# Layer 1's input loaded one layer earlier, and its queries, keys and norms moved from two-bank to one-bank PSUM tiles, in a four-layer network of four images

## The chip, the core and the metric

The kernel runs on one core of one Trainium2 chip. Five engines work in it, each through its own list of instructions in order: PE (matmuls; PEld is its weight loads), DVE, ACT, POOL, and SP, which here only issues DMAs. ACT and POOL issue DMAs too. The metric is the device time of one execution in microseconds (us), as the median of several.

## The reference, cut to what matters

The input is four images of 32 x 32 pixels with 384 channels, in f32. Four layers follow one another, each of them on the group-normalised input (32 groups of 12 channels) and added to it:

```
x = x + L0(gn(x))   # deformable attention: offsets from a convolution, samples of the
                    # image gathered at the offsets, 6 heads over 1024 x 1024 positions
x = x + L1(gn(x))   # 12 heads of 32 channels:
                    #   q, k, v = x Wqkv;  xg = x Wg;  gc = strided 3x3 convolution of xg
                    #   sim = sigmoid(l2norm(xg) . l2norm(gc)),  w = sim sim^T
                    #   softmax(q k / sqrt(32)) * (gamma w + 1 - gamma), renormalised, times v
x = x + L2(gn(x))   # ratio of windowed sums
x = x + L3(gn(x))   # 3x3 local attention: weights from x Wa, values x Wv, folded back
```

## The kernel before, in words

P is 128 partitions, N the 1024 positions of an image, KC = 3 blocks of 128 channels, NJ = 8 blocks of 128 positions.

**Two streams.** `Front` is layer 0, `Trunk` layers 1 to 3 of an image. Both are Python generators that yield a weight after each piece of work. Layer 0 of image 0 runs alone. Then `Net.layer3` drives `Trunk.image(b)` and, by the weights, lets layer 0 of image b+1 advance beside it (1109 units of trunk against 714 of front, with a lead of 0.1). With image 3 there is no front left. This gives the order in which the instructions are written; a scheduler then orders each engine's list by its own estimate of when operands come, except those pinned with `keep_in_program_order` (the first heads, and in a gather the first multiply and the first transpose).

**PSUM.** `big()` gives tiles of two banks, of which there are two buffers; `bank()` gives tiles of one bank, of which there are four. Front and trunk share both. `weights()` (L237) loads a 128 x 3 x 384 weight into one of three buffers.

**Layer 1's inputs** (`inputs1`, from L1059). x is loaded by three DMAs of SP (L1063). The norm takes statistics on DVE (L306, L307), sums them over groups on PE with one-column matmuls (L330, once for the means `gn_mv`, once for the variances `gn_d`) and writes xh (L357). The product with Wg goes by `dense_t` (L376: six matmuls of 512 columns into a big) to the padded tile xp (L1076), from which DVE makes the strided convolution. `queries_keys(ko)` makes one block of q and one of k by `dense_t`, each in a big, copied out whole (L1101 on ACT, L1103 on DVE) and stored to DRAM (L1104). Squares are summed over heads (L1131) and inverted. `sums_step(i)` (L1246, L1254, L1255) makes the maximum and the sum of exponentials of pair 0's softmax for one block of rows; it uses both bigs: matmuls, reduction on DVE, exponential on ACT. The norms (L1158, L1166, L1172) take a big and a bank for each ko, the values (L390, L1110) a bank. `sums_finish` and `load_lse` bring the sums to DRAM and back.

**Layer 1's pairs** (`pair`, six for an image). `sims` makes sim in its own tile (L1285, L1292); then for each of eight blocks POOL scales a part of it to sg (L1350), PE makes q k into a big (L1365), ACT its exponential (L1373), PE the group weights from sim and sg and the transposes of earlier blocks (L1395, L1390), ACT copies what later blocks need (L1403), DVE multiplies (L1404), PE multiplies with the values (L1339).

**Layers 2 and 3.** `layers23` keeps x in a tile of its own. `out1` loads it on ACT's queue (L1438) and adds the projection (L1450, L1462). Layer 2 keeps three tiles d (L1503). Layer 3 has its own xh; each of eight blocks of weights goes to DRAM (L1660) and back skewed as mt (L1662), even ones on SP and odd ones on ACT. x is transposed by PE (L1671) and copied by ACT into eight tiles y (L1675); then PE multiplies mt with the values (L1683), DVE adds y (L1691) and SP stores (L1692).

**The front's parts that matter here.** sidx (L509) holds the indices of the samples. POOL gathers them with 48 indirect DMAs for an image, in eight groups of six (L667), into three buffers gat; DVE weighs and sums a group (L680, L681, L683, the last reader of gat), PE transposes it (L694). POOL's sg of the trunk stand in the same list as the gathers. The convolution of the offsets is L599, its result copied by L607. The first image's heads (`heads0`, L820 on) are a hand-made software pipeline over 96 blocks, all pinned; AHEAD is how many blocks the scores run ahead of the exponentials, and its tiles win, z and lg have 8, 5 and 23 buffers. In a turn DVE does L885 (z), L890 (lg), L935 (adds the scores), L940 (running maximum) and L954 (subtracts it); PE ends a block with L964.

Of the kernel before, what the change touches and what calls it, by code (L numbers as in the profile page):

```python
# [21 lines left out]
ALU = mybir.AluOpType  # L22
# [4 lines left out]
P = 128  # L27
NB, HW, C = 4, 32, 384
N = HW * HW
# [43 lines left out]
class Net:  # L73


    def __init__(self, ctx, tc, a):
        self.tc, self.nc, self.a = tc, tc.nc, a
        nc = self.nc
        pool = lambda name, bufs, **kw: ctx.enter_context(
            tc.tile_pool(name=name, bufs=bufs, **kw)  # L80
        )
        self.const = pool("const", 1)
        self.wts = pool("wts", 3)
        self.ps2 = pool("ps2", 2, space=PSUM)
        self.ps1 = pool("ps1", 4, space=PSUM)
        self.dram = pool("dram", 1, space=DRAM)
        self.n = 0
        self.consts()
        self.scratch()
        self.front, self.trunk = Front(self, "right"), Trunk(self, "left")  # L90

    def nm(self, base):
# [187 lines left out]
class Lane:  # L280
# [32 lines left out]

    def norm(self, x, out, mv=None):


        nc = self.nc
        if mv is None:
            mv = self.moments()
            for k in range(KC):  # L320
                self.stats(mv, x, k)
        gmat = self.weights("gmat")

# [75 lines left out]
class Front(Lane):  # L399
# [419 lines left out]
    def heads0(self, work):  # L819
# [9 lines left out]

        AHEAD, SUB, OUT = 8, 10, 11  # L830
        win, z, lg, ps, half, dens, inv = {}, {}, {}, {}, {}, {}, {}
# [11 lines left out]
        def divide(step, k):  # L843
# [6 lines left out]
            elif step == 1:  # L850
                pin(v.reciprocal(dens[k], dens[k]))
                for r, h in enumerate(heads):
                    nc.sync.dma_start(by_row(self.rden[h]), dens[k][:, r, :])
                for q in range(2):
                    inv[q] = tile_of([P, HN], "lg", 23)
                    for r, h in enumerate(heads):
                        nc.sync.dma_start(
                            inv[q][r * GC : (r + 1) * GC],
                            self.rden[h][0, q * HN : (q + 1) * HN].partition_broadcast(GC),
                        )  # L860
            else:
                for q in range(2):
                    out = queries(2 * k, q)
                    w = inv[q].rearrange("p (y x) -> p y x", x=HW)
                    pin(v.tensor_tensor(out, out, w, ALU.mult))

        def turn(t):
            i = t + AHEAD

            if i + 5 < n:  # L870
                h, q, j = blocks[i + 5]
                win[i + 5] = tile_of([P, (HH + 1) * WROW], "win", 8)
                nc.gpsimd.indirect_dma_start(
# [19 lines left out]
            if 0 <= i < n:  # L893
                lg[i] = tile_of([P, HN], "lg", 23)
                pin(nc.scalar.activation(
# [5 lines left out]
            if 0 <= i + 1 < n:  # L901
                wv = win[i + 1].rearrange("p (r c) -> p r c", c=WROW)
                z[i + 1] = tile_of([P, HH, HW + 1], "z", 5)
                pin(nc.scalar.activation(
# [87 lines left out]
        for i in range(4):  # L992
            h, q, j = blocks[i]
            win[i] = tile_of([P, (HH + 1) * WROW], "win", 8)
            nc.gpsimd.indirect_dma_start(
# [40 lines left out]
class Trunk(Lane):  # L1036


    def image(self, b, out):
        with self.scope("l1y"):  # L1040

# [17 lines left out]
    def inputs1(self, b):  # L1059
        nc, v = self.nc, self.nc.vector  # L1060
        x = self.wt([P, KC, N], "x")
        for k in range(KC):
            nc.sync.dma_start(x[:, k, :], self.x1[b % 2][k * P : (k + 1) * P, :])  # L1063
        xh = self.wt([P, KC, N], "xh")
        self.norm(x, xh)
        yield 15


# [26 lines left out]

        def queries_keys(ko):
            for w, dst in ((wq, self.qd), (wk, self.kd)):
                ps = self.dense_t(w, xh, ko)
                t = self.wt([P, N], "qk", 2)
                if dst is self.qd:  # L1100
                    nc.scalar.mul(t, ps, HD1**-0.5)  # L1101
                else:
                    v.tensor_copy(t, ps)  # L1103
                nc.sync.dma_start(dst[ko * P : (ko + 1) * P, :], t)  # L1104

# [7 lines left out]

        queries_keys(0)
        self.load_sums(0)
# [23 lines left out]
        nc.scalar.activation(inv[:, N:], psc[0 : KC * 32, 0:M1], AF.Sqrt)  # L1139
        queries_keys(1)  # L1140
        yield 14
        wv = self.weights("Wqkv", 2 * C)
        for part in (inv[:, 0:512], inv[:, 512:]):
            v.tensor_scalar(part, part, 1e-12, None, ALU.max)
            v.reciprocal(part, part)
        self.sums_step(0, st)
        queries_keys(2)
        yield 14
        self.sums_step(1, st)
        yield 10  # L1150
        values(range(NJ // 2))
        self.sums_step(2, st)
        yield 18
        for k in range(KC):
            rows, heads = slice(k * P, (k + 1) * P), slice(32 * k, 32 * k + 32)
            ps, pc = self.big(), self.bank()
            for out, lo in ((ps[:, 0:512], 0), (ps[:, 512:N], 512), (pc[:, 0:M1], N)):
                nc.tensor.matmul(  # L1158
                    out,
                    self.hall[heads, :],  # L1160
                    inv[heads, lo : lo + out.shape[-1]],
                    start=True,
                    stop=True,
                )
            t = self.wt([P, N + M1], "sq", 2)
            v.tensor_tensor(  # L1166
                t[:, 0:N].rearrange("p (y x) -> p y x", y=HW),
                pads[k][:, 1:, 1:],
                ps.rearrange("p (y x) -> p y x", y=HW),
                ALU.mult,  # L1170
            )
            v.tensor_tensor(t[:, N:], raw[:, k, :], pc[:, 0:M1], ALU.mult)  # L1172
            nc.sync.dma_start(self.xgd[rows, :], t[:, 0:N])
            nc.sync.dma_start(self.gcd[rows, :], t[:, N:])
            if k == 0:
                self.load_groups(0)
            self.sums_step(3 + k, st)
            yield 8
        for i in range(2):
            values(range(4 + 2 * i, 6 + 2 * i))  # L1180
            self.sums_step(6 + i, st)
        self.sums_finish(0, st)
        self.load_lse(0)
        yield 28

# [90 lines left out]
    def sims(self, p):  # L1276

        nc = self.nc
        sim = self.wt([P, 2, 2, N], "sim")
        for h in range(2):  # L1280
# [147 lines left out]
    def layers23(self, b, out):  # L1428
        with self.scope("l23"):
            self.x = self.wt([P, KC, N], "x")  # L1430
            yield from self.out1(b)
# [35 lines left out]
    def layer2(self):  # L1467
        nc, v = self.nc, self.nc.vector
        with self.scope("l2"):
# [8 lines left out]
            def squares(k):  # L1478
# [23 lines left out]
                t = self.wt([P, HW, HW + 2], "t", 2)  # L1502
                d = self.wt([P, HW, HW], "d", KC)  # L1503
                v.tensor_tensor(t, sq[:, :, 0 : HW + 2], sq[:, :, 1 : HW + 3], ALU.add)
# [60 lines left out]
    def layer3(self, b, out):  # L1565
        nc, v = self.nc, self.nc.vector
        skew = self.skew[b % 2]
        with self.scope("l3"):
# [209 lines left out]
```

## Time and profile before

| what | us |
|---|---|
| median of three runs | 4804.75 (4781.11 to 4805.06) |
| the profiled execution | 4803.82 |
| its span, from first to last instruction | 4802.0 |
| PE busy, DVE busy, ACT busy, POOL busy | 4201.4, 3136.5, 2411.3, 942.6 |
| mean granted clock of PE | 0.917 of full |

| stretch of the span | what runs |
|---|---|
| 0 to 570 | layer 0 of image 0, alone |
| 570.1 | x of layer 1, image 0, is loaded |
| 1776.2, about 2933, 4030.3 | the same of images 1, 2 and 3 |
| 4030 to 4802 | image 3's layers 1 to 3, without a front |

In the profile's views, "[6.44 <-DMA x<-x]" says that the engine was idle 6.44 us before and that a DMA into x ended it; "x12" is a count of instructions put together in a row. `big<-xh,w` names the tile written and the tiles read. In the table of windows each row is a stretch of time with each engine's busy time in it; PEclk is the clock that was granted to PE, 1.00 being full. A matmul leaves two records, its operands being f32: the counts in the views are of records.

### The profile page before, as it was taken

The page shows a single profiled execution, that of the slowest core. Times are in us where ns is not written, and L with a number is a line of the kernel's source. Part 1 is how long each engine was busy: PE and PEld are TensorE (multiplying, and loading weights), DVE is VectorE, ACT ScalarE, POOL GpSimd, SP SyncE. Part 2 cuts the span into 40 slices and gives each one's busy share as a digit, 9 for nine tenths or more (in the row PEclk, how much of TensorE's full clock was granted, in tenths as well). Part 3 has the DMA queues.
Part 4 walks back from the last instruction along what each step waited for, and adds up shares of the span by engine and source line. Part 5 has one row for each costly group of instructions (what it writes and reads, how often), then busy time and mean ns, then how long its engine had stood idle before and what let it go on. Part 6 is the DMA issues. An engine that isn't in the chain of part 4 may idle for free. (4 is left out here: it accounts for less than half of the span.)

```text
span 4802.0 us, 46610 instructions
## 1 busy us (share of the span) xinstructions
PE 4201.4 (87%) x15704; PEld 1793.1 (37%) x15704; DVE 3136.5 (65%) x5727; ACT 2411.3 (50%) x3693; POOL 942.6 (20%) x946
## 2 busy tenths in 40 slices
PE   5477798999999898899999989799999998999988
PEld 2222243333333353333333444343333334343444
DVE  3599655777877727577778744667686873455544
ACT  2166333666665313566767332456676631466642
POOL 0643104211212102311212110421121210000000
PEclk8689897999999987999999989799999998899998
DMA  6433234222212233321212133431121213201011
GB/s 118 142 102 103 81 101 131 84 60 57 71 40 73 75 116 123 106 57 48 80 50 68 44 100 116 130 98 55 38 77 39 79 47 109 86 25 31 19 39 40
DMA packets 230927, 366.82 MB, mean 76 GB/s; under 512 B 117475, under 2 KB 164672, under 8 KB 230688
## 3 DMA queue, kind: packets, MB, share of 16 engines
q1 hardware_dynamic: 169672, 197.36, 13.9%
q0 software_dynamic: 39936, 145.53, 10.3%
q10 hardware_dynamic: 21080, 20.96, 1.8%
q8 instruction: 124, 2.03, 0.2%
q14 instruction: 115, 0.94, 0.1%
HBM read 285.84 MB, written 78.21 MB: 76 GB/s over the span
## 5 line engine op out<-in xcount | busy, mean ns | idle before, releaser
L1404 DVE SCALAR_TENSOR_TENSOR e<-bank,gam,e 128x512 f32<-128x512 f32 x768 | 558.3, 749 | 571.8 <-ACT gn L1403 276.4
L1395 PE MATMUL bank<-sim,sg 128*128 128x512 f32 (+3 forms) x2304 | 877.4, 515 | 11.6 <-POOL sg L1350 8.9
L1255 ACT ACTIVATE big<-big,nmax 128x1024 f32<-128x1024 f32 x384 | 418.6, 1090 | 395.2 <-DVE nmax L1254 340.2
L1373 ACT ACTIVATE e<-big 128x1024 f32<-128x1024 f32 x384 | 376.9, 1019 | 363.4 <-PE big L1365 358.1
L1395 PEld LDWEIGHTS bank<-sim,sg 128*128 128x128 f32 x2304 | 408.3, 200 | 390.5 <-issue 301.4
L1254 DVE TENSOR_REDUCE nmax<-big 128x1 f32<-128x1024 f32 x384 | 453.5, 1218 | 77.0 <-PE big L1246 34.1
L752 POOL DMA_INDIRECT win<-strips,widx x288 | 308.1, 1070 | 629.2 <-DVE z L765 328.1
L1350 POOL TENSOR_SCALAR sg<-sim,gam 128x512 f32<-128x512 f32 x192 | 148.5, 776 | 1430.8 <-PE bank L1395 1140.7
L1365 PE MATMUL big<-qa,ka 64*128 64x512 f32 x1536 | 414.1, 630 | 14.8 <-ACT big L1255 8.8
L1246 PE MATMUL big<-k,q 32*128 32x512 f32 x1536 | 355.2, 697 | 81.4 <-ACT big L1255 38.2
L667 POOL DMA_INDIRECT gat<-pairs,sidx x192 | 210.1, 1094 | 500.6 <-DVE ix_gt L479 401.7
L773 PE MATMUL bank<-qpad,kz 128*128 128x512 f32 x576 | 283.0, 617 | 15.0 <-DVE e L1404 15.0
L808 PE MATMUL bank<-lg,va 128*64 128x512 f32 x576 | 265.0, 602 | 16.3 <-ACT lg L806 16.2
L808 PE MATMUL bank<-lg,ones 128*64 128x512 f32 x576 | 264.3, 602 | 0.0
L770 DVE SCALAR_TENSOR_TENSOR lg<-z,bias_f,lg 128x512 f32<-128x512 f32 x288 | 227.9, 803 | 40.1 <-ACT lg L769 38.6
L764 ACT ACTIVATE z<-win,bias_f 128x528 f32<-128x528 f32 x288 | 207.1, 739 | 63.3 <-DVE lg L770 39.2
L1365 PEld LDWEIGHTS big<-qa,ka 64*128 64x128 f32 x1536 | 135.5, 189 | 272.4 <-issue 159.3
L765 DVE SCALAR_TENSOR_TENSOR z<-win,bias_f,z 128x528 f32<-128x528 f32 x288 | 216.2, 769 | 27.0 <-DMA win<-strips,widx 16.6
L805 DVE TENSOR_TENSOR lg<-lg,tb 128x512 f32<-128x512 f32 x288 | 187.6, 705 | 51.4 <-ACT tb L798 51.4
L1339 PE MATMUL bank<-e,vs 128*32 128x512 f32 x1536 | 210.9, 605 | 2.1 <-DVE vs L1333 2.1
L769 ACT ACTIVATE lg<-z,bias_f 128x512 f32<-128x512 f32 x288 | 201.4, 720 | 19.1 <-PE bank L808 10.7
L376 PE MATMUL big<-xh,w 128*128 128x512 f32 x432 | 199.3, 619 | 12.2 <-ACT big L1255 10.8
(291 smaller groups left out, 6658.3 us busy)
## 6 DMA issues: line engine op xcount, KB each, us to landing
pairs<-xn SPq DMA_DIRECT2D x64, 192.0 KB
q<-qd SPq DMA_DIRECT2D x48, 256.0 KB
w<-in_gmat SPq DMA_DIRECT2D x16, 576.0 KB
w<-in_w_off SPq DMA_DIRECT2D x12, 576.0 KB
w<-in_Wqkv SPq DMA_DIRECT2D x12, 576.0 KB
a<-in_x SPq DMA_DIRECT2D x16, 384.0 KB
x<-a ACTq DMA_DIRECT2D x4, 1536.0 KB
win<-strips,widx POOLq DMA_INDIRECT x384
```

Of the source, the lines that this page charges most:

```text
L752: nc.gpsimd.indirect_dma_start(out=win, out_offset=None, in_=self.strips[:, :], in_offset=bass.IndirectOffsetOnAxis(ap=self.widx[:, q, c : ...
L765: v.scalar_tensor_tensor(z, wv[:, 1 : HH + 1, 0 : HW + 1], sc(0, 1), z, ALU.mult, ALU.add)
L770: v.scalar_tensor_tensor(lg, z[:, :, 1 : HW + 1], sc(0, 0), lg, ALU.mult, ALU.add)
L773: nc.tensor.matmul(ps, kz[:, j * P : (j + 1) * P], both, start=True, stop=True)
L808: nc.tensor.matmul(po[out, :], w, lf, start=j == 0, stop=j == NJ - 1)
L1246: nc.tensor.matmul(ps[r][:, h * 512 : (h + 1) * 512], self.q4[rows, i * P : (i + 1) * P], self.k4[rows, 0:512], start=True, stop=True,)
L1254: v.tensor_reduce(nmax[:, r, i : i + 1], ps[r], AX.X, ALU.max, negate=True)
L1255: nc.scalar.activation(ps[r], ps[r], AF.Exp, bias=nmax[:, r, i : i + 1], accum_out=den[:, r, i : i + 1],)
L1365: nc.tensor.matmul(ps[:, r, :], ka[rows, j * P : (j + 1) * P], qa[rows, cols], start=True, stop=True,)
L1373: nc.scalar.activation(e, ps, AF.Exp)
L1395: nc.tensor.matmul(ps[:, (mid - i0) * P :], sg[:, r, m, :], sim[:, r, m, mid * P : i1 * P], start=m == 0, stop=m == 1,)
L1404: v.scalar_tensor_tensor(e[:, r, :], ps, self.gam[:, 1:2], e[:, r, :], ALU.add, ALU.mult, accum_out=tot[:, r, h : h + 1],)
```

## The change

A pool `keep` at the bottom of the trunk's stack holds one tile "whole" of 16 KB a partition. It serves in turn as layer 1's x, normed in place, as the tile of the sims of each pair, and as x of layers 2 and 3; its last quarter is the third d of layer 2, which has two buffers d left.

`Trunk.start` loads x and gmat. For image 0 it runs at its start, for the others within layer 3 of the image before, behind the transposes of x; the norm then stands at the start of `image`, ahead of the scope of layer 1.

`product` makes one block of q or of k in two single banks, each copied out by itself; products, sums steps and values are interleaved in another order (a product after each of the first sums steps, one block of values after each of the later ones, and the last three behind `sums_finish`). The norms of a ko take three single banks. The matmuls are the same in number; ACT has 12 instructions more and DVE 24.

Layer 3's y lie in the memory of its xh. The first heads run 5 blocks ahead instead of 8, with 6, 4 and 20 buffers win, z and lg.

```diff
--- before
+++ after
@@ -88,6 +88,7 @@
...
         self.front, self.trunk = Front(self, "right"), Trunk(self, "left")
+        self.trunk.work = self.trunk.keep = pool("keep", 1, side="left")
@@ -319,7 +320,8 @@
...
                 self.stats(mv, x, k)
-        gmat = self.weights("gmat")
+        if gmat is None:
+            gmat = self.weights("gmat")
@@ -827,7 +829,7 @@
...
-        AHEAD, SUB, OUT = 8, 10, 11
+        AHEAD, SUB, OUT = 5, 10, 11
         win, z, lg, ps, half, dens, inv = {}, {}, {}, {}, {}, {}, {}
@@ -869,7 +871,7 @@
...
                 h, q, j = blocks[i + 5]
-                win[i + 5] = tile_of([P, (HH + 1) * WROW], "win", 8)
+                win[i + 5] = tile_of([P, (HH + 1) * WROW], "win", 6)
                 nc.gpsimd.indirect_dma_start(
@@ -900,7 +902,7 @@
...
                 wv = win[i + 1].rearrange("p (r c) -> p r c", c=WROW)
-                z[i + 1] = tile_of([P, HH, HW + 1], "z", 5)
+                z[i + 1] = tile_of([P, HH, HW + 1], "z", 4)
                 pin(nc.scalar.activation(
@@ -1036,7 +1038,28 @@
...
+    def whole(self):
+        work, self.work = self.work, self.keep
+        t = self.wt([P, 4 * N], "whole")
+        self.work = work
+        return t, t[:, 0 : KC * N].rearrange("p (k n) -> p k n", k=KC)
+    def start(self, b):
+        x = self.whole()[1]
+        for k in range(KC):
+            self.nc.sync.dma_start(x[:, k, :], self.x1[b % 2][k * P : (k + 1) * P, :])
+        self.begun = x, self.weights("gmat")
     def image(self, b, out):
+        if b == 0:
+            self.start(b)
+        x, gmat = self.begun
+        self.norm(x, x, None, gmat)
+        self.xh = x
+        yield 15
         with self.scope("l1y"):
@@ -1058,13 +1081,7 @@
...
         nc, v = self.nc, self.nc.vector
-        x = self.wt([P, KC, N], "x")
-        for k in range(KC):
-            nc.sync.dma_start(x[:, k, :], self.x1[b % 2][k * P : (k + 1) * P, :])
-        xh = self.wt([P, KC, N], "xh")
-        self.norm(x, xh)
-        yield 15
+        xh = self.xh
@@ -1093,15 +1110,24 @@
...
-        def queries_keys(ko):
-            for w, dst in ((wq, self.qd), (wk, self.kd)):
-                ps = self.dense_t(w, xh, ko)
-                t = self.wt([P, N], "qk", 2)
+        def product(w, ko, dst):
+            t = self.wt([P, N], "qk", 2)
+            for h in range(2):
+                ps, out = self.bank(), t[:, h * 512 : (h + 1) * 512]
+                for ki in range(KC):
+                    nc.tensor.matmul(
+                        ps,
+                        w[:, ki, ko * P : (ko + 1) * P],
+                        xh[:, ki, h * 512 : (h + 1) * 512],
+                        start=ki == 0,
+                        stop=ki == KC - 1,
+                    )
                 if dst is self.qd:
-                    nc.scalar.mul(t, ps, HD1**-0.5)
+                    nc.scalar.mul(out, ps, HD1**-0.5)
                 else:
-                    v.tensor_copy(t, ps)
-                nc.sync.dma_start(dst[ko * P : (ko + 1) * P, :], t)
+                    v.tensor_copy(out, ps)
+            nc.sync.dma_start(dst[ko * P : (ko + 1) * P, :], t)
@@ -1111,7 +1137,9 @@
...
-        queries_keys(0)
+        product(wq, 0, self.qd)
+        product(wk, 0, self.kd)
         self.load_sums(0)
@@ -1137,50 +1165,49 @@
...
         nc.scalar.activation(inv[:, N:], psc[0 : KC * 32, 0:M1], AF.Sqrt)
-        queries_keys(1)
+        product(wq, 1, self.qd)
         yield 14
-        wv = self.weights("Wqkv", 2 * C)
         for part in (inv[:, 0:512], inv[:, 512:]):
...
         self.sums_step(0, st)
-        queries_keys(2)
+        product(wk, 1, self.kd)
         yield 14
         self.sums_step(1, st)
-        yield 10
-        values(range(NJ // 2))
+        product(wq, 2, self.qd)
+        wv = self.weights("Wqkv", 2 * C)
+        yield 14
         self.sums_step(2, st)
-        yield 18
+        product(wk, 2, self.kd)
+        yield 14
         for k in range(KC):
+            self.sums_step(3 + k, st)
             rows, heads = slice(k * P, (k + 1) * P), slice(32 * k, 32 * k + 32)
-            ps, pc = self.big(), self.bank()
-            for out, lo in ((ps[:, 0:512], 0), (ps[:, 512:N], 512), (pc[:, 0:M1], N)):
+            t = self.wt([P, N + M1], "sq", 2)
+            parts = [(N, M1, raw[:, k, :], t[:, N:])]
+            for h in range(2):
+                out = t[:, h * 512 : (h + 1) * 512].rearrange("p (y x) -> p y x", x=HW)
+                parts.append((h * 512, 512, pads[k][:, 1 + 16 * h : 17 + 16 * h, 1:], out))
+            for at, n, src, out in parts:
+                ps = self.bank()[:, 0:n]
                 nc.tensor.matmul(
-                    out,
-                    self.hall[heads, :],
-                    inv[heads, lo : lo + out.shape[-1]],
-                    start=True,
-                    stop=True,
-                )
-            t = self.wt([P, N + M1], "sq", 2)
-            v.tensor_tensor(
-                t[:, 0:N].rearrange("p (y x) -> p y x", y=HW),
-                pads[k][:, 1:, 1:],
-                ps.rearrange("p (y x) -> p y x", y=HW),
-                ALU.mult,
-            )
-            v.tensor_tensor(t[:, N:], raw[:, k, :], pc[:, 0:M1], ALU.mult)
+                    ps, self.hall[heads, :], inv[heads, at : at + n], start=True, stop=True
+                )
+                if at < N:
+                    ps = ps.rearrange("p (y x) -> p y x", x=HW)
+                v.tensor_tensor(out, src, ps, ALU.mult)
             nc.sync.dma_start(self.xgd[rows, :], t[:, 0:N])
...
                 self.load_groups(0)
-            self.sums_step(3 + k, st)
+            values(range(k, k + 1))
             yield 8
         for i in range(2):
-            values(range(4 + 2 * i, 6 + 2 * i))
             self.sums_step(6 + i, st)
+            values(range(3 + i, 4 + i))
         self.sums_finish(0, st)
         self.load_lse(0)
+        values(range(5, NJ))
         yield 28
@@ -1276,7 +1303,7 @@
...
         nc = self.nc
-        sim = self.wt([P, 2, 2, N], "sim")
+        sim = self.whole()[0].rearrange("p (r m n) -> p r m n", r=2, m=2)
         for h in range(2):
@@ -1427,7 +1454,8 @@
...
         with self.scope("l23"):
-            self.x = self.wt([P, KC, N], "x")
+            whole, self.x = self.whole()
+            self.spare = whole[:, KC * N :].rearrange("p (y x) -> p y x", y=HW)
             yield from self.out1(b)
@@ -1500,7 +1528,7 @@
...
                 t = self.wt([P, HW, HW + 2], "t", 2)
-                d = self.wt([P, HW, HW], "d", KC)
+                d = self.wt([P, HW, HW], "d", 2) if k < 2 else self.spare
                 v.tensor_tensor(t, sq[:, :, 0 : HW + 2], sq[:, :, 1 : HW + 3], ALU.add)
@@ -1664,17 +1692,19 @@
...
             values(range(NJ // 2, NJ))
-            ys = []
+            ys = self.wt([P, KC, N], "xh").rearrange("p k (a c) -> p (k a) c", c=P)
+            ys = ys.rearrange("p (i k) c -> p i (k c)", k=KC)
             for i in range(NJ):
...
                     )
-                y = self.wt([P, C], "y", NJ)
-                nc.scalar.copy(y, pt[:, 0:C])
-                ys.append(y)
+                nc.scalar.copy(ys[:, i], pt[:, 0:C])
             yield 20
+            if b + 1 < NB:
+                self.start(b + 1)
             for i in range(NJ):
@@ -1687,7 +1717,7 @@
...
                     )
-                y = ys[i]
+                y = ys[:, i]
                 v.tensor_tensor(y, ps[:, 0:C], y, ALU.add)
```

More of the change, by code (lines that the diff above doesn't have):

```diff
@@ L312, in moments, with norm @@
         return self.wt([P, KC, 2], "gn_mv", 2)
-    def norm(self, x, out, mv=None):
+    def norm(self, x, out, mv=None, gmat=None):
         nc = self.nc
@@ L854, in divide @@
                 for q in range(2):
-                    inv[q] = tile_of([P, HN], "lg", 23)
+                    inv[q] = tile_of([P, HN], "lg", 20)
                     for r, h in enumerate(heads):
@@ L893, in turn @@
             if 0 <= i < n:
-                lg[i] = tile_of([P, HN], "lg", 23)
+                lg[i] = tile_of([P, HN], "lg", 20)
                 pin(nc.scalar.activation(
@@ L993, in heads0 @@
             h, q, j = blocks[i]
-            win[i] = tile_of([P, (HH + 1) * WROW], "win", 8)
+            win[i] = tile_of([P, (HH + 1) * WROW], "win", 6)
             nc.gpsimd.indirect_dma_start(
```

## The prediction

> **What bounds the kernel now.** I read the windows first (busy time by stage), then the timeline where PE falls idle, then the gathers' tile. The page gives PE 87% of the span, so the places that matter are those where PE is not busy or not at full clock.
>
> The windows; the columns are the stretch, its length, then the busy time of PE, PEld, DVE, ACT and POOL, the granted clock, the DMA share and GB/s:
>
> ```profile
> 716.00:800.00 84.00, 63.42 (x163) 25.45 (x162) 49.49 (x68) 33.29 (x51) 54.78 (x50) 0.70 0.55 165
> 1865.00:1952.00 87.00, 64.17 (x158) 24.97 (x157) 49.49 (x66) 32.74 (x50) 51.90 (x49) 0.65 0.51 158
> 4027.00:4046.00 19.00, 7.22 (x31) 6.41 (x29) 6.60 (x17) 1.55 (x2) 8.22 (x16) 0.62 0.29 106
> 4046.00:4160.00 114.00, 104.48 (x265) 41.62 (x265) 50.29 (x59) 39.46 (x61) 0.00 (x0) 0.86 0.35 112
> ```
>
> Rows one and two are images 0 and 1 while layer 0's gathers of the next image run: PE lacks 21 and 23 us and has 0.70 and 0.65 of its clock. Row three is the boundary between images 2 and 3, row four layer 1's inputs of image 3, with no front left to fill in.
>
> Timeline of that boundary:
>
> ```profile
> 4030.30 1.27 SPq L1063 DMA_DIRECT2D x<-x  x3
> 4034.65 1.28 DVE L306 BATCH_NORM_STATS2 gn_st<-x 128x6 f32<-128x512 f32 x2 [6.44 <-DMA x<-x]
> 4036.39 0.56 PE L330 MATMUL bank<-gn_mv,w 128*128 128x1 f32 x2 [8.85 <-DMA x<-x]
> 4037.63 2.83 PE L330 MATMUL bank<-gn_mv,w 128*128 128x1 f32 x12 [0.68 <-DVE gn_mv L307]
> 4041.30 3.15 PE L330 MATMUL bank<-gn_d,w 128*128 128x1 f32 x14 [0.84 <-DVE gn_d L347]
> 4045.86 2.08 PE L376 MATMUL big<-xh,w 128*128 128x512 f32 x2 [1.41 <-DVE xh L357]
> ```
>
> The last L1683 matmul ends about 4027.5, the first product L376 starts at 4045.86: 18.3 us, of which the load and the statistics are the first half.
>
> The tile gat in 1865 to 1960: who kept POOL from its next gather (us, times):
>
> ```profile
> L667 POOL DMA_INDIRECT gat<-pairs,sidx x48: 945/949/2223, 1865.9 to 1950.7; - x48
>   DVE xn L683: 20.5, 2
>   issue: 13.1, 43
> ```
>
> L683 is the last reader of a gat buffer: DVE frees the buffers late. And for the first heads, DVE in 400 to 430:
>
> ```profile
> 400.00:430.00 30.00, 21.24 (x58) 5.95 (x58) 29.72 (x46) 19.32 (x30) 12.02 (x10) 0.89 0.36 100
> ```
>
> DVE is busy 29.72 of 30 us: that stage is DVE's.
>
> **Part 1, the boundary 2 to 3.** In the changed order SP issues the three x loads after the first output store (one store instead of eight stand ahead; the seven others queue behind three short issues of 0.4 us). The loads wait for the last transposes L1671, done about 4015, so land by about 4020 (4030.30 to 4034.65 was 4.35 us). Six statistics of 0.65 (4 us) stand on DVE between the additions L1691 and are done about 4026, while the L1683 matmuls run to 4028. What follows the last L1683: 2.83 + 0.84 + 3.15 + about 1.4 for reciprocal and first xh = 9 us. 18.3 becomes about 9: **−9**. Between −4 (statistics or additions get in each other's way) and −12 (the half clock, 0.50 from 4035 to 4050, shortens too).
>
> Boundaries 0 to 1 and 1 to 2: there the front fills PE, and L330 waited only 4.25 and 3.9 us. Against that, the y copies L1675 now write into the memory of layer 3's xh, after its last readers, and on ACT they stand behind the mt loads (1729.04 to 1734.08; the last SP part lands about 1743). PE's new order has a first L1683 and transposes ahead of twelve L376 and 36 conv matmuls L599 that before came first (L1683 began at 1750.99). So a wait of 7 to 10 us appears and about 8 go (L330, and part of the half clock): **0**, within 4 each way.
>
> **Part 2, layer 1's inputs of image 3.** From 4045.86 to the first L1365 at 4163.60: 117.7 us. Full-clock work of PE in it: 54 product matmuls x 0.86 = 46, 24 of values x 0.65 = 16, eight sums steps x 1.13 = 9, norms and squares 12, sims 4: 87 us. The missing 30 are waits for the two bigs and the clock of 0.86 that comes of them. A big is freed by:
>
> ```profile
> L1254 DVE TENSOR_REDUCE nmax<-big 128x1 f32<-128x1024 f32 x10 | 12.0, 1221 | 8.1 <-PE big L1246 8.1
> L1255 ACT ACTIVATE big<-big,nmax 128x1024 f32<-128x1024 f32 x10 | 10.9, 1089 | 18.5 <-DVE nmax L1254 18.4
> L1166 DVE TENSOR_TENSOR sq<-xp,big 128x1024 f32<-128x1024 f32 x3 | 3.7, 1222 | 9.2 <-PE big L1158 9.2
> ```
>
> (groups by line, 4120 to 4163). A sums step holds both bigs for 1.1 (matmul) + 2 x 1.2 (reduce) + 1.1 (exp), about 5 us. Before, products and norms queued for the same two bigs; now they have the four single banks and lie beside the steps. Chain: products and convolution as before, then steps 0 to 3 each covered by a product, steps 4 to 7 at 5 us each with norms and values beside them: about 97 us. **−20**, between −10 (the banks become the queue) and −26 (all but 4 us of the waits). The split costs 12 ACT and 24 DVE instructions: a half costs 0.585 on ACT (the 128x512 copies L1403) for 1.02 whole, 0.684 on DVE (128x512 from a bank, L774) for 1.22, so 0.15 us more for each pair; DVE is busy 50 and ACT 39 of 114 us, so this is hidden; uncovered it is 9 pairs x 0.15, 1.4 us an image. The first sim of pair 0 now waits for the last values matmuls (same tile): 9 L390 of 0.65, 6 us, counted in the chain.
>
> **Part 3, the gather stages of images 0 to 2.** From sidx to the first sg (POOL, behind the 48th gather): 78.7, 86.3 and 79.4 us (716.7 to 795.4, 1865.4 to 1951.7, 3022.3 to 3101.7). POOL's waits beyond its own issue: 10.8 (put down to qa<-lse), 20.5, and 11.1 + 1.4. Take them away and 67.9, 65.8 and 66.9 are left: a floor of gather issue, three times the same. In the changed order the reductions L680 to L683 stand earlier among the steps on DVE (groups 1 and 2 at once, 3 after norms 0, 1 and step 4, then 4 to 7), and the steps no longer wait for a product to leave a big. All of it would be 10.8 + 20.5 + 12.5 = 44. By my chain groups 3 and 4 still lose 2 to 4 us per image to the norms and steps ahead of them: **−36**, between −44 and, if DVE frees buffers as late as now, 0; a loss is the rival below. PE sits idle or at half clock here, so what sg gains the pair loop gains.
>
> One row speaks to the clock. In 1785 to 1795 PE was busy 10.00 of 10.00 us at a granted clock of 0.50; in 1880 to 1920, 28.05 of 40 us, 0.50 throughout. The Trainium skill ("TensorE: Matmul & The Clock Gate", section "What's actually happening") gives half clock after about 3.4 us idle and full clock after about 3.4 us busy. By that rule every gap taken away would give back at most some 2 us beyond itself; this trace pays for longer, up to 10 us of busy time at half speed. I leave both out of the sum, as part of the range.
>
> **Part 4, the first heads.** From 310 to 520 DVE runs 63 turns (63 additions L954) in 210 us: 3.33 each. Running 5 instead of 8 blocks ahead takes three turns out of PE's tail, where a block is four L964 records of 0.603, 2.4 us, into the DVE stage: 3 x 0.93 = **+2.8**. Below: −2, since the DVE prologue is shorter; above: +8, if window buffers (6 for 8) or lg (20 for 23) make POOL's loads late: now POOL is busy 12.02 of 30 us, with gathers issued five turns, 16 us, ahead, against the 7 us that a gather took to land.
>
> **Part 5, x of layers 2 and 3.** Its load (L1438, ACT queue) now waits for the last reader of the sims, L1395 at 4650.6, instead of being issued at 4648.3; on ACT only a y copy and the next norm's scaling are behind it. Use is at 4661.6: 11 us for 4.35 us of landing, so 0; if it were late, 2 to 3 us in each of four images.
>
> **Sum**: −9 + 0 − 20 − 36 + 2.8 = −62. The span of 4802.0 and 1.8 around it make the profiled run 4803.8, 1 under the median of 4804.75; 4803.8 − 62 = **4742**.
>
> **Rivals.**
> A. The gathers keep their stage: buffers come free as late as now, because norms and steps still precede group 3 on DVE. Then part 3 gives 0 to −10: 4803.8 − 9 − 20 + 2.8 − 5 = **4773**. For: DVE has 49 of 87 us busy, so order decides and not load. Against: the three waits that I can subtract leave the same floor.
> B. Slower: the new order makes the trunk's steps wait for gathers. DVE is in order, so steps 3 to 7 stand behind L680 of groups 1 to 4; if a buffer's landing is late, sums, lse and sg all slip. Its place is DVE's queue between sidx and group 4. At 14 us per group (as in the two spells that waited for L683) sidx to sg is 14.5 + 7 x 14 = 112 us, +26 to +33 in each of three images, about 90 in all: 4803.8 − 9 − 20 + 2.8 + 90 = about **4868**. It decides once groups come more than about 10 us apart (14.5 + 70 = 84, where nothing is gained), against 7.5 us of issue.
> C. More: all 44, the boundary at −12, inputs at −26, and recovered half clock of some 15 with the first heads unchanged at +2.8: 4803.8 − 12 − 44 − 26 + 2.8 − 15 = about **4710**.
>
> **Chances.** Forecast case (4720 to 4765) 0.57; A (4765 to 4790) 0.21; B 0.12; C 0.10. About 0.5%, 24 us, is what a measurement here can tell from no change. Faster by over that (below 4780): 0.57 + 0.10 + two thirds of A = 0.81; within, the rest of A: 0.07; slower, B: 0.12. Range: from C with the first heads at their lower bound, −2, which is 4705, to near A's end, 4786, which leaves B and scraps out.
>
> **What would show it.** Right: at the last boundary the x load is issued about 4016 on the old clock and L376 follows the last L1683 by 9 us; POOL's waits for xn L683 in the gather stages fall under 5 us, with sidx to sg under 72; inputs to first L1365 under 100 in image 3; L1246's waits there only for L1255 in the last four steps. Wrong: POOL waits for L683 again, or the steps' reduces L1254 show idle time from gat; ACT idle behind mt in the boundaries 0 to 1 and 1 to 2 by over 10 us; DVE under 29 of 30 us in the first heads; L1462 waiting for x.

## The result, and the profile after

The changed kernel takes 4759.5 us (median of six, 4747.02 to 4762.87), the kernel before beside it 4799.59: a ratio of 0.9916, 95% interval 0.9896 to 0.9937. That is 40 us less, where 62 were forecast. The profiled execution took 4762.87 us with a span of 4761.1, against 4803.82 and 4802.0.

The two traces, laid side by side at the same instructions, give where the 40.9 us of span came from:

| stretch | forecast | measured |
|---|---|---|
| start, and the first heads to the last L964 | +2.8 | −1.0, then +4.3 |
| from there to sidx of image 0's stage | 0 | −2.7 |
| boundaries 0 to 1 and 1 to 2 (out1 to sidx) | 0 | −8.5 and −5.4 |
| gather stages, images 0, 1, 2 (sidx to first sg) | −36 | −0.3, −6.7, +3.2 |
| boundary 2 to 3 (last mt matmul to first product) | −9 | −12.5 |
| image 3's inputs (first product to first q k) | −20 | −18.2 |
| pair loops and layers 2 and 3, the rest | 0 | +7 |

The last row is what the others leave of −40.9. The boundary 2 to 3 in the timeline of after, PE and DVE and the load:

```profile
4004.07 1.27 SPq L1053 DMA_DIRECT2D whole<-x  x3
4007.85 1.27 DVE L307 BATCH_NORM_STATS2 gn_st<-whole 128x6 f32<-128x512 f32 x2
...
4016.13 1.62 PE L332 MATMUL bank<-gn_mv,w 128*128 128x1 f32 x14
...
4018.60 1.72 PE L332 MATMUL bank<-gn_d,w 128*128 128x1 f32 x14 [0.84 <-DVE gn_d L349]
...
4022.09 12.49 PE L378 MATMUL big<-whole,w 128*128 128x512 f32 x22 [1.77 <-DVE whole L359]
```

The last L1713 ends at 4016.30, the first product starts 5.8 us later; it was 18.3. The load is issued 12 us before that end, the statistics run among the additions, and the one-column matmuls take 1.62 and 1.72 where they took 0.56 + 2.83 and 3.15, at half clock (0.50 from 4035 to 4050 before).

The windows of after that answer to those shown of before (same columns; the last row is the first heads):

```profile
717.00:797.00 80.00, 56.55 (x164) 23.98 (x163) 47.97 (x70) 31.02 (x51) 52.56 (x50) 0.77 0.58 183
1856.00:1937.00 81.00, 57.98 (x166) 24.26 (x164) 48.34 (x71) 30.92 (x51) 54.67 (x50) 0.77 0.57 181
4022.00:4121.00 99.00, 94.77 (x273) 39.15 (x273) 52.09 (x65) 42.09 (x65) 8.49 (x16) 0.97 0.38 129
400.00:430.00 30.00, 24.14 (x62) 7.27 (x62) 28.93 (x45) 19.69 (x31) 11.88 (x10) 0.83 0.31 93
```

In image 3's inputs PE works at 0.97 of its clock in 99 us, before at 0.86 in 114. In the gather stages PE still lacks 23 of 80 us.

### The profile page after: what moved, and what is told of

Same layout as the page of the kernel before. It is cut to its first block, busy times and chain, and to the rows that moved or that the text cites. A ratio compares the mean times of both kernels' runs of the same rounds, so it can differ in the third digit from the quotient of the medians.

```text
span 4761.1 us, 46669 instructions
## 1 busy us (share of the span) xinstructions
PE 4167.2 (88%) x15704; PEld 1779.4 (37%) x15704; DVE 3137.8 (66%) x5751; ACT 2415.4 (51%) x3705; POOL 949.3 (20%) x946
## 4 chain that ended last, share of the span: by engine, by line
PE 36%; ACT 8%; DVE 8%; issue 3%; DMA 2%; POOL 0%; another core or an unknown queue 0%; SPq 0%; ACTq 0%; DVEq 0%; POOLq 0%
PE bank L1422 8%; PE big L1392 4%; PE big L1273 3%; PE bank L810 3%; PE bank L775 2%; PE bank L392 2%; PE bank L1366 2%; PE bank L1417 2%; PE big L378 2%; ACT big L1282 2%; DVE nmax L1281 1%; DVE e L1431 1%; PE big L1312 1%; ACT e L1400 1%; PE big L1545 1%
## 5 line engine op out<-in xcount | busy, mean ns | idle before, releaser
L1422 PE MATMUL bank<-whole,sg 128*128 128x512 f32 (+3 forms) x2304 | 878.2, 515 | 2.8 <-DVE e L1431 2.8
L1422 PEld LDWEIGHTS bank<-whole,sg 128*128 128x128 f32 x2304 | 408.3, 200 | 383.8 <-issue 303.8
L1281 DVE TENSOR_REDUCE nmax<-big 128x1 f32<-128x1024 f32 x384 | 453.0, 1218 | 66.2 <-PE big L1273 30.1
L1377 POOL TENSOR_SCALAR sg<-whole,gam 128x512 f32<-128x512 f32 x192 | 151.0, 789 | 1405.6 <-PE bank L1422 1142.4
L1273 PE MATMUL big<-k,q 32*128 32x512 f32 x1536 | 333.3, 690 | 104.8 <-ACT big L1282 40.4
L771 ACT ACTIVATE lg<-z,bias_f 128x512 f32<-128x512 f32 x288 | 201.6, 720 | 18.2 <-PE bank L810 9.6
L776 DVE TENSOR_TENSOR lg<-bank,lg 128x512 f32<-128x512 f32 x288 | 192.5, 684 | 19.8 <-PE bank L775 17.1
```

The lines of the kernel that those rows point to most:

```text
L1273: nc.tensor.matmul(ps[r][:, h * 512 : (h + 1) * 512], self.q4[rows, i * P : (i + 1) * P], self.k4[rows, 0:512], start=True, stop=True,)
L1281: v.tensor_reduce(nmax[:, r, i : i + 1], ps[r], AX.X, ALU.max, negate=True)
L1422: nc.tensor.matmul(ps[:, (mid - i0) * P :], sg[:, r, m, :], sim[:, r, m, mid * P : i1 * P], start=m == 0, stop=m == 1,)
```

## The experiments

The twelve experiments ran in three series of four, each with the kernel before beside it; ratios are to that kernel. It took 4765 us in the first series, 4801 in the second and 4768 in the third, so times of different series are not compared; stretches of the traces are. The record names another chip for each series (12, 15 and 7) and none for the runs of the prediction.

**Five gather buffers.**

```diff
+        extra = self.wt([P, 2, G, 2, 2 * GC], "a12", 2)
         xsT = self.wt([P, KC, N], "a12", 2)
...
+            if j in (3, 4):
+                gat = extra[:, j - 3]
+            else:
+                gat = self.wt([P, G, 2, 2 * GC], "gat", 3)
```

> The changed kernel with two more buffers for the gathers of layer 0: groups 3 and 4 of eight go into a tile that lies in memory that is free then (the 12 KB of layer 0's normalised offsets); nothing else is edited. Theory 1 (the gather stages of images 0 to 2 gained nothing because POOL still waits for L685 to free gat: 30.1 us in all): these waits go, sidx to the first sg falls from 78.4, 79.6 and 82.6 us to about 68, and the time falls by 10 for each image, to about 4730 us. Theory 2 (the stage is set by PE, which is at half clock there and stands in order behind the transposes L696): POOL's waits go, but the pair loop starts no earlier, 4755 to 4765.

Measured: 4720.94, ratio 0.9900 (0.9884 to 0.9915), sidx to sg 67.4, 67.9 and 69.0 us. But the next experiment, with three buffers, has 67.2, 68.0 and 67.9 in the same series. So the buffers did nothing here, and the stage is 11 to 14 us shorter than in the profile of after for another reason.

**The load at the image's start.** In the program's text only:

```diff
-        if b == 0:
-            self.start(b)
+        self.start(b)
...
-            if b + 1 < NB:
-                self.start(b + 1)
```

> The changed kernel with x of layer 1 loaded at the start of each image again instead of within layer 3 of the image before; tiles, banks and orders of inputs1 stay as changed. Theory 1 (the early load gives 12.5 us at the boundary 2 to 3, where the gap before the first product fell from 18.3 to 5.8, and takes the 4 us wait of the norm's first matmul and the half clock after it away at the boundaries 0 to 1 and 1 to 2, 8 and 5 us): 25 us slower than the changed kernel, about 4785. Rival (the two front-covered boundaries gained by the new order around the mt wait, not by the load): only 10 to 12 us slower, 4770.

Measured: 4726.09, ratio 0.9913 (0.9899 to 0.9928), no slower. The trace shows why: the first two x loads are issued at 3965.72, before the last matmuls of layer 3, as in the changed kernel. The place in the text does not matter here; the load goes out once x is transposed and its tile is free, the last transpose ending at 3965.69. The experiment undid nothing, so neither theory is tested by it. It serves below as the changed kernel in that series.

**Inputs as before.** From `wq, wk` on, `inputs1` is that of before; early load and one tile stay. The core of the edit:

```diff
-        def product(w, ko, dst):
...
+        def queries_keys(ko):
+            for w, dst in ((wq, self.qd), (wk, self.kd)):
+                ps = self.dense_t(w, xh, ko)
...
+            ps, pc = self.big(), self.bank()
...
-                ps = self.bank()[:, 0:n]
```

> The changed kernel with the products, norms, values and sums steps of layer 1's inputs as before: products in bigs, norms in a big and a bank, the old order; early load and one tile stay. Theory 1 (small banks pay only where no gathers run): image 3's inputs go from 99.5 back to 118 us, gather stages within 5 us of the changed kernel's, together about 4780. Rival (the small banks also keep the gather stages from getting worse, since the norms no longer hold a big): 10 us more in each of images 0 to 2, about 4805.

Measured: 4754.93, ratio 0.9975 (0.9966 to 0.9983). From the last mt matmul to the first q k of image 3 it is 124.6 us, against 106.6 in the experiment before this: +18. The gather stages are 69.8, 70.2 and 71.7 against 67.2, 68.0 and 67.9: +2.6, +2.2, +3.8. Together 27 us, and the difference of the ratios is 0.0062 of 4765, 30 us. Theory 1 holds; the small banks and the new order, which this edit undoes together, are worth 18 us without gathers and some 3 an image with them. Which of the two gives how much was not separated.

**The first heads' sizes alone**, on the kernel before:

```diff
-        AHEAD, SUB, OUT = 8, 10, 11
+        AHEAD, SUB, OUT = 5, 10, 11
```

and win 6, z 4, lg 20 as in the change.

> The kernel before with the new sizes of the first heads alone (5 blocks ahead for 8; win 6, z 4, lg 20). Theory 1 (three turns go from PE's tail into the stretch that DVE sets): the last L964 ends 4 us later than before (547.8), the whole 3 to 4 us slower, about 4803. Rival (the sizes cost nothing; the 4 us come of where the pools lie): within 1 us of before.

Measured: 4772.8, ratio 1.0013 (1.0004 to 1.0022), 2 to 10 us slower; the last L964 ends at 552.25 for 547.79. Theory 1.

**The kernel before, again**, with no edit.

> The kernel before, unedited, for its trace on the chip of this call. In the experiment with the first heads' sizes (all but the kernel before) the gather stages took 69.7, 71.0 and 70.8 us from sidx to sg, against 78.7, 86.3 and 79.4 in the profile the prediction was made from. Theory 1 (that profile held stalls of its execution or its chip, not of the code): about 70 us here too. Rival (the sizes of the first heads move the pools and so the gathers): 78 to 86 us.

Measured: 4800.82 us; sidx to sg 83.5, 85.8 and 85.0 us. The numbers are the rival's, its cause is not: the changed kernel, with the small sizes, has long stages in this series too (next). The stage takes 70 us in one series and 84 in another; what differs in the traces is shown three experiments further down.

**The changed kernel, again**, with no edit.

> The changed kernel, unedited, on the chip of this call. Theory 1 (what the gather stages gain is small, 2 to 4 us an image, since their floor of 67 us was 70 before already): 0.990 to 0.992 of before; sidx to sg 67 to 69 us where before has 70. Rival (the gain depends on the chip's stalls): with before at 70, more than 1% faster.

Measured: 4761.77, ratio 0.9913 (0.9897 to 0.9929), stages 81.6, 76.9 and 79.5 us beside the 83.5, 85.8 and 85.0: −2, −9, −6. The ratio is theory 1's, the stages are not: here they gain 16 us together, in the first series 8.

**The load held back.**

```diff
         x = self.whole()[1]
+        if y is not None:
+            self.nc.vector.tensor_copy(x[:, :, 0:1], y[:, 0:KC].unsqueeze(2))
...
-            if b + 1 < NB:
-                self.start(b + 1)
...
+                if i == NJ - 1 and b + 1 < NB:
+                    self.start(b + 1, y)
```

> The changed kernel with the x load of the next image held back until the last addition of layer 3: one 128x3 copy by DVE from the last sum into the tile that the load writes, and the statistics behind it. All else stays. (The experiment that only moved the load in the program's text left it early: its tile is free once x is transposed.) Theory 1 (the early load gives all of the gain at the boundaries): 10 to 12 us more at 2 to 3, and 8 and 5 at 0 to 1 and 1 to 2, 0.5% slower than the changed kernel. Rival (at the boundaries with a front the order of L599 and L1713 gave the gain): 10 to 12 us in all, 0.25% slower.

Measured: 4781.74, ratio 0.9950 (0.9931 to 0.9969), beside 0.9913: 18 us slower by the medians' ratios. In the traces the gap at 2 to 3 is 16.0 us for 7.0, and from out1 to the end of the offsets' convolution it is 253.6 and 254.0 us for 244.1 and 244.2: 9 to 10 us at each of the three. That is 28 us in the traces; the 18 us by the ratios lie between the two theories, and their intervals leave 6 to 30. The two boundaries with a front lose as much as the one without, which is theory 1; the order alone gave nothing, since the kernel before has 248.6 and 248.8 us there in this series.

**Five buffers beside the changed kernel**, the edit as in the first experiment.

> The changed kernel with five gather buffers for three, beside the changed kernel on the same chip. Theory 1 (where the stage runs at POOL's own pace no gather waits for a buffer): within 2 us of the changed kernel if its sidx to sg is 67 to 69 us, and 8 to 10 us an image better if it is 78 or more. Theory 2 (PE sets the stage): no gain in either case.

Measured: 4793.41, ratio 0.9984 (0.9967 to 1.0001), against 0.9913. Theory 1 falls, and theory 2's "no gain" is met, though it foresaw no loss: the stages are 92, 95 and 95 us, longer with more buffers. The waits of ACT and DVE from sidx of image 0's stage on, of this kernel (us in all, times, longest):

```profile
ACT vn L1140 <- remote: 21.6, 1, 21.6
...
ACT big L1286 <- issue: 8.1, 2, 5.8
...
DVE nmax L1285 <- remote: 6.7, 1, 6.7
```

and its timeline there:

```profile
755.92 4.21 PE L392 MATMUL bank<-w,whole 128*128 128x384 f32 x6 [0.28 <-issue]
...
772.39 2.48 PE L392 MATMUL bank<-w,whole 128*128 128x384 f32 x4
...
781.42 0.95 POOL L673 DMA_INDIRECT gat<-pairs,sidx  x1 [0.30 <-issue]
785.63 0.48 ACT L1140 COPY vn<-bank 128x384 f32<-128x384 f32 x1 [21.63 <-remote]
785.76 2.35 DVE L1285 TENSOR_REDUCE nmax<-big 128x1 f32<-128x1024 f32 x2 [6.71 <-remote]
786.01 0.48 ACT L705 COPY a<-bank 128x384 f32<-128x384 f32 x1
```

The values' matmuls are recorded up to 774.87, PE then shows nothing until 788.34, and ACT and DVE, whose operands come from PE, start together at 785.6, 4 us after the last gather was issued at 781.42. The block of values that ACT copies at 785.63 is the one recorded from 755.92 to 760.13, 25 us before. In the trace's semaphore events, PE's five results arrive between 785.61 and 785.85; the one before them came at 775.09. The profile models the ends of matmuls, so it does not tell whether PE worked late or its results were signalled late. Waits over 2 us on PE, ACT and DVE that the profile puts to "issue" or "remote" (leaving out the lines L330, L548, L699 and L1088 of before and their like, which show such rows outside these stages too) come to 188 us in this trace, to 91, 90 and 131 in the three others of this series (before, changed, load held back), and to 109 and 117 in the profiles of before and after that the prediction and the result rest on. In the first series they are 0 in the runs with five and with three buffers, 25 with the old inputs and 11 with the heads' sizes alone.

**Two buffers.**

```diff
-            gat = self.wt([P, G, 2, 2 * GC], "gat", 3)
+            gat = self.wt([P, G, 2, 2 * GC], "gat", 2)
```

> The changed kernel with two gather buffers for three, so that the gathers of images 0 to 3 come less densely. What five buffers did: 67 to 69 us from sidx to sg where no unexplained waits stand (first call), but 92 to 95 us where they do (second call, changed kernel 77 to 82): there PE's matmuls are recorded as done and DVE and ACT, which wait for them, start up to 25 us later, until the gathers have been issued. Theory A (dense gathers hold PE's results up): fewer or shorter such waits, sidx to sg 75 to 85 us in either state. Theory B (buffers as such set the stage): 8 us more than the changed kernel for each image, about 0.5% slower than it, the waits for L685 twice as long.

Measured: 4756.21, ratio 0.9977 (0.9968 to 0.9986). This series, too, has no unexplained waits, so theory A got no test. From sidx to the start of pair 1 each image loses 8 to 11 us against the first series's run with three buffers (stages 74.3, 73.7 and 76.5 us), and the first image's gathers lose 7: theory B.

**Direct transfers for gathers.**

```diff
+            if b:
+                for g in range(G):
+                    at = j * G + g
+                    nc.gpsimd.tensor_copy(gat[:, g, 0, 0:1], sidx[:, at : at + 1])
+                    row = pairs[g * SLOTS + j * P : g * SLOTS + j * P + P, :]
+                    nc.gpsimd.dma_start(
+                        gat[:, g].rearrange("p l c -> p (l c)"),
+                        bass.AP(row.tensor, row.offset, [[2 * GC, P], [1, 4 * GC]]),
+                    )
+                return gat
```

> The changed kernel with the indirect gathers of images 1 to 3 replaced by direct transfers of as many bytes from the unshifted rows, issued by POOL as before, each behind a one-column copy that reads sidx (the samples are thus not at the offsets). Theory A (what holds PE's results up comes of the indirect form): no unexplained wait over 3 us in the three stages, sidx to sg under 55 us, 12 to 25 us less for each image. Theory C (it comes of the bytes written beside the sums steps, or of PE itself): the waits stay, and sidx to sg within 8 us of the changed kernel.

Measured: 4724.06, ratio 0.9916 (0.9899 to 0.9932), stages 68.1, 66.9 and 63.4 us. POOL's waits in image 0's stage, of this kernel:

```profile
POOL gat L670 <- DVE sidx L511: 135.7, 1, 135.7
POOL gat L670 <- DVE xn L695: 26.6, 4, 11.5
POOL gat L672 <- DMA gat<-pairs: 3.4, 4, 1.2
POOL sg L1387 <- ACT whole L1329: 1.8, 1, 1.8
```

A transfer now takes POOL 0.54 us for 0.95 and 0.30 between two, and POOL merely waits 26.6 us more for the buffers that L695 frees. So two chains end at about 67 us in an undisturbed stage. With indirect gathers POOL issues almost without a break (in the first series's run with three buffers, image 0: 52.4 us busy, 13.1 between the issues); with a cheaper issue DVE's release of the buffers takes as long. What sets that second chain was not tested. Theory C, as far as the length goes; on the unexplained waits this series says nothing.

**The front further ahead, and further behind** (0.2, then 0.04):

```diff
-TRUNK_STEPS, FRONT_STEPS, LEAD = 1109.0, 714.0, 0.1
+TRUNK_STEPS, FRONT_STEPS, LEAD = 1109.0, 714.0, 0.2
```

> The changed kernel with LEAD 0.2 for 0.1: layer 0 of images 2 and 3 runs further ahead, so that their gathers stand beside the products with Wg and the squares and not beside the sums steps; image 1 keeps its place only in part. Theory A or B (the gathers cost because reductions and steps stand in one list with them on DVE): images 1 and 2 gain 5 to 15 us each in this stretch, the changed kernel less 10 to 25 us, about 0.986 of before. Rival (the front's work is only moved, and what it filled before is now bare: the end of layer 3 and the pairs of the image): as the changed kernel, 0.991, or slower.

> The changed kernel with LEAD 0.04: the gathers stand in the loop of pair 0, behind layer 1's inputs. Theory A or B: inputs without gathers take 100 us as in image 3, and the gathers in pair 0 wait for nothing that PE needs soon; 10 to 25 us less than the changed kernel, 0.986 of before. Rival (pair 0 has DVE busy with L1431 and both bigs in use by L1392 and L1273, so that the gathers' L682 to L685 delay each turn): 0.991 or slower.

Measured: 4867.87, ratio 1.0215 (1.0201 to 1.0229), and 4786.39, ratio 1.0045 (1.0031 to 1.0059). Both rivals, worse than put. Further ahead, PE waits 57.9 us for L685 between 700 and 900 us, in four waits, the longest 31.6. Where the rest of the loss lies, and why the other lead loses, was not followed up.

## Why the prediction was right and wrong

The sign, the range and "faster by over 0.5%" held, but the sum of −62 was made of parts of which the largest did not come. That the time still lies in the forecast case is luck in part: 14 us came at the boundaries 0 to 1 and 1 to 2, which I had put at 0, and without them the profiled run would have been 4776.8, in the band of rival A. The experiments that undo or add one part each account for the whole: the early load is worth 18 us by the ratios (0.0037), the inputs' banks and order 30 (0.0062), and the sizes of the first heads cost 6 (0.0013). Together that is 42 us for the 40 measured, the first two with intervals of some 12 and 8 us.

- **The boundary 2 to 3: right, a little small.** −12.5 for −9, just past the end of the range that I gave to the clock. The terms that I kept at 2.83 and 3.15 shrank to 1.62 and 1.72, at full clock, and the first of them began before the last L1713 ended.
- **Image 3's inputs: right.** −18.2 for −20, and the reversal of this part alone costs 18 us. PE's waits there fall from 11 to 6 us, and in the windows shown PE is busy for 95 us instead of 104: more of the gain is in the clock than in the waits themselves.
- **The gather stages: wrong.** The step that failed is "Take them away and 67.9, 65.8 and 66.9 are left: a floor of gather issue", and the −36 that follows. The floor is real: undisturbed, the changed kernel runs the stage in 67 to 68 us. But the same series has it at about 70 with the inputs of before, where POOL waits 1.0, 3.6 and 3.5 us for L683; so the change is worth 3 us an image, 8 in all. POOL in image 1's stage of that series, with the heads' sizes alone and then in the run that serves as the changed kernel:

```profile
L667 POOL DMA_INDIRECT gat<-pairs,sidx x48 | 52.9, 1103 | 98.2 <-DVE ix_gt L479 80.6 <-issue 13.4 <-DVE xn L683 3.6
```

```profile
L669 POOL DMA_INDIRECT gat<-pairs,sidx x48 | 53.2, 1107 | 77.8 <-DVE sidx L511 63.4 <-issue 13.4 <-DVE gat L683 0.3
```

So most of the 44 us that I subtracted were not the order's. These waits stand in traces where PE's results reach DVE late, and DVE's reductions L680 to L683 stand in its list behind steps that wait for those results; so it is after the change too, where POOL waits for L685 again, 30.1 us in all, which was my mark of an error. My profile held such a disturbance, and I took its whole cost for the price of the old order. A second sign was there: idle times of DVE and ACT in these stages that the profile put to "issue" and "remote" and not to any instruction. Of before, in 1860 to 1955:

```profile
ACT big L1255 <- issue: 13.7, 4, 7.0
...
DVE nmax L1254 <- remote: 5.8, 2, 5.6
```

- Rival A's outcome thus came for these stages, but not its cause: it wasn't norms and steps ahead of group 3.
- **The boundaries 0 to 1 and 1 to 2: wrong, to the good.** "A wait of 7 to 10 us appears and about 8 go": the wait for mt is 3.6 us, and what goes is more than the wait of L330. The two waits, before and then after:

```profile
1782.22 0.55 PE L330 MATMUL bank<-gn_mv,w 128*128 128x1 f32 x2 [4.25 <-issue]
```

```profile
1735.31 1.62 PE L1713 MATMUL bank<-vals,mt 128*128 128x384 f32 x2 [3.56 <-DMA mt<-skew]
```

One pair of windows shows it, before and then after, over 1781 to 1798:

```profile
1781.00:1798.00 17.00, 15.78 (x64) 8.42 (x66) 6.45 (x17) 1.54 (x2) 3.56 (x11) 0.53 0.17 54
```

```profile
1781.00:1798.00 17.00, 17.00 (x109) 7.96 (x109) 4.90 (x9) 1.60 (x4) 9.75 (x16) 1.00 0.29 90
```

Before, a gap of 4.25 us was followed by 17 us at half clock, though PE was busy in all but 1.2 of them. After, there is no gap in these windows and the clock stays at 1.00; the wait for mt is followed by 6.8 us at half clock. With the load held back PE waits 2.8 us there and the granted clock is 0.5 for 13.7 us again. I had left this out of the sum, "as part of the range"; yet 17 us at half clock are, by an estimate from this row, up to 8.5 us of work lost, twice the wait in front of them. The Trainium skill ("TensorE: Matmul & The Clock Gate", section "What's actually happening") lets the clock return after at least one window, about 3.4 us, of sustained work. Here it took 13.7 and 17 us of matmuls with one-column ones among them, and 6.8 us behind the wait for mt, where there were none, so one window is too little to reckon with in this kernel. That the half clock follows idle time, as the page says, these three places agree with. In the changed kernel of the second series 3.4 us at half clock follow the one-column matmuls without a PE wait in front of them, so idle time is not all of it.
- **The first heads: right mechanism, +4.3 for +2.8.** The sizes alone cost 2 to 10 us. DVE is busy 28.93 of 30 us in the window that I had named, just under the 29 that I had set as the mark of an error; the smaller buffers seem to cost a little beside the three turns, which no run separates. The 7 us that I gave a gather to land were too long: by the semaphore events of before, most of these gathers land about 3.8 us after their issue.
- **x of layers 2 and 3: right.** L1490 waits for L1478's matmuls alone, 33.9 us in all against 33.8 before, and never for the load.
- **Open:** what holds PE's results back in the second series and in the runs of the prediction. Nearly all of it lies beside gathers, it is longer when they are denser (90 to 131 us with three buffers, 188 with five), and with five buffers the last late result of the three stages comes 4.2, 3.0 and 1.9 us after the last gather is issued. Whether it is the indirect form, POOL's issue or the writes was not settled: the run with direct transfers fell into a series without it. Nor is it known what differs between the series: all four traces of chip 15 have it, while on chips 12 and 7 at most 5.5 us of such waits fall in the three stages of a trace; but each chip served in one series only, so chip and moment are not separated.

## What to carry to other kernels

A wait that a profile shows is worth its length only if the change removes what causes it: before a wait for a buffer is booked as a gain, follow it one step further, to what made the releasing engine late, and be wary where that ends at "issue" or "remote". Here a load moved by its tile's memory being free, not by its line in the program. And a PE gap of 3 to 4 us cost what it lasted plus the half clock behind it, here 7 to 17 us at half speed, the longer in front of one-column matmuls, so such gaps are worth more than they look.

## What the runs showed of the hardware

In one of the three series and in the runs of the prediction, PE's results beside dense gathers reached ACT and DVE late, by up to 25 us after the matmuls were recorded, five at once within 0.25 us. Five gather buffers for three then made the stage 10 to 18 us longer, and in an undisturbed series changed nothing. An indirect gather of 128 rows took POOL 0.95 us and 0.30 between two, a direct transfer of as many bytes from POOL 0.54.
